# Emitting the pooling of an image one operation at a time, and new durations in the account that orders the work

## The chip, the cores and the metric

The kernel runs on one core of a Trainium2 chip. The metric is the device time of one execution in microseconds (us), as the median of several executions. For the kernel before it is 3456.73 us, from three executions between 3454.76 and 3458.35 us.

## What is computed

The input is a batch of 8 images of 256 channels and 32 x 32 pixels, all in 32-bit floats. Two layers follow one another; each adds its result to its input.

```
x = x + L0(groupnorm(x))       # layer 0: attention over pooled keys
t = tokens(x)                  # (8, 1024, 256)
t = t + attn(layernorm(t))     # layer 1: one head of 256
t = t + experts(layernorm(t))  # 8 experts, three products each, weighted by a gate
```

Layer 0 is where the change sits. Its keys and values are not those of the pixels but of four pooled maps of the image:

```
for i, r in enumerate([1, 2, 3, 6]):          # 32x32, 16x16, 11x11, 5x5
    p = einsum('bchw,ph,qw->bcpq', t, Mh, Mw) # means over windows
    p = p + depthwise3x3(p, w[i], b[i])
```

The four maps have 1024 + 256 + 121 + 25 = 1426 places. After a layer norm they are the keys and values of 8 heads of 32 channels, and the 1024 queries of an image attend to all of them. Pooling and the projection to keys and values commute, so the kernel pools the image itself and projects afterwards.

## The kernel before, in words

**The steps of attention.** For each image, each half of the heads (four heads, side by side in the array of TensorE), each half of the queries (512) and each of 12 chunks of keys, the kernel makes one *step*: 8 x 2 x 2 x 12 = 384 steps. `scores` makes four matmuls of 32 rows into a PSUM tile `sc` of four banks, of which there is one, and one exponential on ScalarE (ACT) of 128 x 2048 values into a buffer `pt`, of which there are six. `values` makes four matmuls of 32 columns from the `pt` of the step before into `pv`. After every second step, `add` (L1459) issues a transfer on the queue of GpSimd (POOL) that adds the second `pt` of a pair onto the first in memory; this is called an *adding transfer* below. A full one moves 1 MB. `sums` then adds the pairs together on VectorE (DVE), for the denominators of the softmax. A `pt` buffer is free again only when its transfer has landed and, for the first of a pair, when DVE has read it.

**The work between the steps.** Everything else runs between the steps: loading and normalising the next image, its pooling, the projections (`maps`), the depthwise taps on DVE (`convolve`), the transposes and norms of keys and values, the output projection, and all of layer 1's attention. Each of these is a generator, called a thread here. A thread yields what its next instructions need: an engine, the tiles that they read, and a PSUM tag. The work of `prepare` for an image (norm, `pool_levels`, `maps`, queries) is one thread, so what follows the pooling cannot be emitted before it. Matmuls emitted between steps by these threads are called *filler* below, since they fill TensorE (PE) while ACT works on the exponential.

**The account that sets the order.** The class `Flow` records every instruction as it is emitted (all instructions go through one helper and so show line L669 in the profile) and ties it to the one before on its engine, so that the emitted order is the order on the chip. `note` (L738) keeps an account of when each engine is next free, with the durations that `cost` (L710) gives, and of when each tile is ready. After each `scores` and after each `values`, `step` (L834) resumes every thread that is `runnable` (L807). For an engine other than PE that is the case if

```
now <= pe + AHEAD[engine]   if the inputs are ready on that engine by then
at  <= pe + NEAR[engine]    otherwise (at: when the inputs are ready)
```

where `now` is the account's time of that engine and `pe` that of PE. Filler for PE is also held to a credit: `PACE` 4.0 us a step, `PACE1` 2.0 us for the threads of layer 1. The account is not consulted on the chip; it only decides the order.

**The pooling.** `pool_levels` (L1273) makes, for each of the two halves of an image's channels, the 16 x 16 map (three operations on POOL) and the 11 x 11 map (seven). A thread yields once before each of these two groups (L1284 and L1290), and so the three, and then the seven, are emitted in one go, without an adding transfer between them. The 5 x 5 map is made by DVE (from L1304 on) in a tile `t5`, which uses the same buffer as the tiles `t2` and `t3` of the POOL operations.

**After attention.** The last of layer 1 is emitted between the first expert products; then the experts run to the end. The first products of an expert are made as plain matmuls while layer 1 is still going on, and by a scheme with seven products in place of eight afterwards.

Of the kernel before, what the change touches and what calls it, by code (L numbers as in the profile page):

```python
# [20 lines left out]
DH = 32  # L21
# [10 lines left out]
CAP = (1.5, 1.5)  # L32
NEVER = 1e9
MARGIN = 1.5
AHEAD = {"DVE": 4.0, "ACT": 2.0, "POOL": 4.0, "SP": 10.0}
NEAR = {"DVE": 1.5, "ACT": 2.0, "POOL": 1.5, "SP": 10.0}
BUFS = {"sm": 2, "sx": 1}
PACE2 = 8.0
LANDING = 9.5
# [12 lines left out]
class Kit:  # L52


    def __init__(self, nc):
        self.nc = nc
        self.n = 0
# [598 lines left out]
class Flow:  # L656
# [18 lines left out]
    def __init__(self, tc, kit):  # L675
        nc = tc.nc
        self.tc, self.kit = tc, kit
        self.now = dict.fromkeys(("PE", "DVE", "ACT", "POOL", "SP"), 0.0)
        self.last = {}
        self.ready, self.read, self.writer, self.reader, self.slots, self.open = {}, {}, {}, {}, {}, set()  # L680
        self.pe = self.Engine(self, "PE", nc.tensor)
        self.ve = self.Engine(self, "DVE", nc.vector)
        self.act = self.Engine(self, "ACT", nc.scalar)
        self.pool = self.Engine(self, "POOL", nc.gpsimd)
        self.sp = self.Engine(self, "SP", nc.sync)
        self.threads = []
        self.cut = {}
        self.also = {}
        self.credit, self.port = [0.0, 0.0], 0.0

    def tile(self, pool, shape, tag, bufs=1):
# [18 lines left out]
    def cost(self, engine, op, out, ins):  # L710
        n = 1
        for s in (out.shape if op != "bn_stats" else ins[0].shape)[1:]:
            n *= s
        if op == "tensor_reduce":
            n = 1
            for s in ins[0].shape[1:]:
                n *= s
        if "dma" in op:
            return 1.0 if engine == "POOL" else 0.4
        if engine == "PE":  # L720
            if op == "transpose":
                return 0.13
            c = max(0.2, 0.00169 * n)
            return c / 4 + 0.05 if ins[0].shape[0] <= DH or ins[0].shape[1] <= DH else c
        psum = any(i.space == PSUM for i in ins)
        if engine == "ACT":
            return 0.2 + 0.00087 * n
        if engine == "POOL":
            if n <= 64 and op == "tensor_tensor":
                return 0.3 + 0.17 * n if n <= NKC else 0.3  # L730
            return 0.15 + (0.0023 if op == "tensor_tensor" else 0.0015) * n
        if op == "reciprocal":
            return 0.1 + 0.0064 * n
        if op in ("tensor_scalar", "tensor_copy") and not psum:
            return 0.14 + 0.00065 * n
        return 0.15 + 0.00107 * n

    def note(self, engine, op, ins, args, kwargs):  # L738
        aps = [a for a in (*args, *kwargs.values()) if hasattr(a, "tensor") or hasattr(a, "space")]
        out = kwargs.get("out", args[0] if args else aps[0])  # L740
        srcs = [a for a in aps if a is not out]
        prev = self.last.get(engine)
        if prev is not None:
            self.tc.add_manual_dep(
                ins.ins,
                prev,
                mybir.DependencyInfo(mybir.DependencyClass.NoSync, mybir.DependencyReason.DATA),
                reason="program order",
            )
        self.last[engine] = ins.ins.name  # L750
        start = self.now[engine]
        names = [n for a in srcs for n in self.keys(a)]
        outs = self.keys(out)
        for n in (*names, *outs):
            if self.writer.get(n) != engine:
                start = max(start, self.ready.get(n, 0.0))
        for o in outs:
            if self.reader.get(o, engine) != engine:
                start = max(start, self.read.get(o, 0.0))
        cost = self.cost(engine, op, out, srcs)  # L760

        wide = [a for a in srcs if a.space != PSUM and a.free_size() > 4]
        if "dma" not in op and engine == "POOL" or engine == "DVE" and wide and (len(wide) > 1 or op in ("tensor_scalar", "tensor_copy")):
            start = max(start, self.port)
            self.port = start + cost
        self.now[engine] = end = start + cost
        lag = 0.15
        if "dma" in op:
            lag = 3.0 if engine == "SP" else LANDING
        for n in {*outs, self.key(out)}:  # L770
            self.ready[n] = max(self.ready.get(n, 0.0), end + lag)
            self.writer[n] = "DMA" if "dma" in op else engine
        self.open.difference_update(names)
        for n in {*names, *map(self.key, srcs)}:
            self.read[n] = max(self.read.get(n, 0.0), end + lag)
            self.reader[n] = engine
# [30 lines left out]
    def runnable(self, need, rank=0):  # L807
# [16 lines left out]
        now = self.now[engine]  # L824
        return now <= pe + AHEAD[engine] if at <= now + 0.3 else at <= pe + NEAR[engine]

# [38 lines left out]
def attention(tc, kit, f, outer, ended, nb, consts, x, t1, t2, hn, bounds, vecs, q_t, kv_t, proj_t, gqk_t, wqk, wqkv, vecs1, w1_d, w1c, gate_d, wrc, vecs2, bnvec):  # L865
# [6 lines left out]
    with ExitStack() as ctx:  # L872
# [5 lines left out]
        def T(pool, shape, tag, bufs=1):  # L878
            return f.tile(pool, shape, tag, bufs=bufs)
# [161 lines left out]
        def ve(*tiles):  # L1041
            return "DVE", tiles, None
# [4 lines left out]
        def pool(*tiles):  # L1047
            return "POOL", tiles, None
# [224 lines left out]
        def pool_levels(xi, xl):  # L1273

            img = xi.rearrange("p k (h w) -> p k h w", h=32)

            def level(s):
                n = SIDES[s]
                return xl[:, :, OFFS[s] - HW : OFFS[s] - HW + n * n].rearrange("p k (h w) -> p k h w", h=n)

            for k in range(2):
                one, l2, l3 = img[:, k], level(1)[:, k], level(2)[:, k]

                yield pool(xi)  # L1284
                t2 = T(work, [P, 32, 16], "pool")
                f.pool.tensor_tensor(t2, one[:, :, 0::2], one[:, :, 1::2], ALU.add)
                f.pool.tensor_tensor(l2, t2[:, 0::2, :], t2[:, 1::2, :], ALU.add)
                f.pool.tensor_scalar(l2, l2, 0.25, 1.0, ALU.mult, ALU.mult)

                yield pool(xi)  # L1290
                t3 = T(work, [P, 32, 11], "pool")
                f.pool.tensor_tensor(t3, one[:, :, 0::3], one[:, :, 1::3], ALU.add)
                f.pool.tensor_tensor(t3[:, :, 0:10], t3[:, :, 0:10], one[:, :, 2::3], ALU.add)
                f.pool.tensor_tensor(t3[:, :, 1:11], t3[:, :, 1:11], one[:, :, 2::3], ALU.add)
                f.pool.tensor_tensor(l3, t3[:, 0::3, :], t3[:, 1::3, :], ALU.add)
                f.pool.tensor_tensor(l3[:, 0:10, :], l3[:, 0:10, :], t3[:, 2::3, :], ALU.add)
                f.pool.tensor_tensor(l3[:, 1:11, :], l3[:, 1:11, :], t3[:, 2::3, :], ALU.add)
                flat = xl[:, k, OFFS[2] - HW : OFFS[3] - HW]
                f.pool.tensor_tensor(flat, flat, con[:, K_S11 : K_S11 + 121], ALU.mult)

            t5 = T(work, [P, 2, 32, 5], "pool")
            ends = [(i * 32 // 5, -(-(i + 1) * 32 // 5)) for i in range(5)]
            for i, (a, e) in enumerate(ends):
                yield ve(xi)  # L1304
                f.ve.tensor_reduce(t5[:, :, :, i], img[:, :, :, a:e], AX.X, ALU.add)
            yield ve(t5, xl)
            l5 = level(3)
            for i, (a, e) in enumerate(ends):
                f.ve.tensor_reduce(
                    l5[:, :, i, :], t5[:, :, a:e, :].rearrange("p k h w -> p k w h"), AX.X, ALU.add  # L1310
                )
            flat = xl[:, :, OFFS[3] - HW :]
            f.ve.tensor_tensor(flat, flat, con[:, None, K_S5 : K_S5 + 25].to_broadcast([P, 2, 25]), ALU.mult)
            pooled.append(True)

        def prepare(b):
# [32 lines left out]
            if b == 0:  # L1349
                f.spawn(pool_levels(xi, xl), 2)  # L1350
            else:
                yield from pool_levels(xi, xl)
# [435 lines left out]
        for i in range(len(steps) + 1):  # L1788
            if i < len(steps):
                b, c, half, kc = steps[i]  # L1790
# [653 lines left out]
```

## Time and profile before

| | before |
|---|---|
| time, median of 3 | 3456.73 us |
| span of the profiled execution | 3452.0 us |
| work ahead of the first step | 0 to 102 us |
| the 384 steps | 102 to 2020 us |
| last of layer 1, with the first expert products | 2020 to 2345 us |
| the other expert products | 2345 to 3452 us |
| adding transfers | 192; 160 of them move 1024 KB each, and land 7.2 us after their issue (median) |
| pooling on POOL, one image | 20 operations of 0.4 to 2.0 us |

A line of a wait reads: who waited, for whom, total us, times, longest us. A line of a timeline reads: start, duration, engine, operation, tiles written and read, shape, how many were merged, and in brackets the idle time of the engine before and what ended it. In a line of windows each engine's busy time is followed by its instructions in brackets.

### The profile page before, as it was taken

Reading aid. Unit: us, or ns where it says so; the run is one execution under the profiler, and the core shown is the slowest. Engines: PE = TensorE matmul, PEld = TensorE weight load, DVE = VectorE, ACT = ScalarE, POOL = GpSimd, SP = SyncE. Lnnn points to the kernel's source line nnn. Section 1 sums busy time; section 2 is a strip of 40 time slices with the busy share of each in tenths; the row PEclk is TensorE's granted clock in tenths of the full one; section 3 lists DMA queues with packets and bytes.
Section 4 is the critical chain, followed back from the end, with each engine's and each line's share of the span. In section 5 each row is a group of like instructions: output and inputs, shape, how many; then the busy total and the mean of one; then the engine's idle time right before and its main releaser. Section 6 shows DMA issues by size and latency. Waiting matters only on the chain.

```text
span 3452.0 us, 39939 instructions
## 1 busy us (share of the span) xinstructions
PE 3212.7 (93%) x15276; PEld 1785.8 (52%) x15276; DVE 2286.3 (66%) x3922; ACT 1673.9 (48%) x2195; POOL 496.1 (14%) x616
## 2 busy tenths in 40 slices
PE   7788889979989899999989989999999999999998
PEld 3322234425434344434434446746777777777776
DVE  6686877787888788787654534316776666666665
ACT  3566666556666566566655533342223333333332
POOL 2113131131141221321121200004000000000000
PEclk9789999999999999999999999999999999999999
DMA  1346655554554565655565754124430001000000
GB/s 48 75 102 155 144 117 111 131 132 98 137 128 101 127 135 130 137 128 121 117 143 128 150 158 164 61 79 141 140 122 19 19 19 37 19 19 19 19 13 20
DMA packets 103881, 333.28 MB, mean 97 GB/s; under 512 B 12848, under 2 KB 38200, under 8 KB 80448
## 3 DMA queue, kind: packets, MB, share of 16 engines
q0 software_dynamic: 24576, 172.51, 25.5%
q1 hardware_dynamic: 75744, 156.16, 13.2%
q8 instruction: 122, 2.00, 0.2%
q10 hardware_dynamic: 3360, 1.97, 0.2%
q14 instruction: 79, 0.65, 0.1%
HBM read 96.23 MB, written 61.87 MB: 46 GB/s over the span
## 4 chain that ended last, share of the span: by engine, by line
PE 73%; DVE 10%; DMA 6%; ACT 5%; issue 3%; POOL 2%; ACTq 0%; SPq 0%; POOLq 0%; DVEq 0%
PE bank L669 24%; PE sm L669 17%; PE y L669 11%; PE sc L669 8%; PE sx L669 6%; PE pv L669 6%; ACT pt L669 4%; DVE acc L669 4%; DMA pt<-pt 3%; DVE pt L669 1%; DVE rec L669 1%; DMA hn<-pool 1%; DMA t<-xr 1%; POOL pool L669 1%; DMA xr<-in_x_dram 1%
## 5 line engine op out<-in xcount | busy, mean ns | idle before, releaser
L669 ACT ACTIVATE pt<-sc 128x2048 f32<-128x2048 f32 (+1 forms) x384 | 720.4, 1876 | 348.0 <-PE sc L669 258.4
L669 PE MATMUL sc<-q,kn 32*128 32x512 f32 (+1 forms) x3072 | 458.3, 667 | 124.2 <-ACT pt L669 123.1
L669 DVE SCALAR_TENSOR_TENSOR acc<-p,vec,acc 128x225 f32<-128x225 f32 (+7 forms) x928 | 530.4, 578 | 39.6 <-ACT acc L669 14.9
L669 PE MATMUL bank<-h,w2e 128*128 128x512 f32 x1024 | 478.4, 593 | 0.0
L669 ACT ACTIVATE h<-bank,bnvec 128x512 f32<-128x512 f32 x298 | 229.5, 771 | 481.6 <-PE bank L669 481.6
L669 DVE TENSOR_TENSOR pt<-pt,pt 128x1024 f32<-128x1024 f32 x320 | 384.7, 1246 | 85.1 <-DMA pt<-pt 68.4
L669 PE MATMUL pv<-pt,vt 128*32 128x512 f32 (+1 forms) x3072 | 424.4, 625 | 0.0
L669 ACT ACTIVATE h<-c,bnvec 128x512 f32<-128x512 f32 x214 | 162.5, 807 | 323.2 <-DVE c L669 323.2
L669 POOL DMA_DIRECT2D pt<-pt x192 | 169.3, 882 | 975.8 <-ACT pt L669 833.5
L669 PEld LDWEIGHTS sc<-q,kn 32*128 32x128 f32 (+1 forms) x3072 | 119.1, 183 | 315.8 <-ACT pt L669 214.2
L669 DVE TENSOR_TENSOR c<-p1c,bank 128x512 f32<-128x512 f32 x107 | 73.5, 687 | 313.7 <-PE bank L669 313.7
L669 PEld LDWEIGHTS bank<-h,w2e 128*128 128x128 f32 x1024 | 194.5, 190 | 150.6 <-issue 138.1
L669 PEld LDWEIGHTS pv<-pt,vt 128*32 128x32 f32 (+1 forms) x3072 | 61.3, 109 | 311.1 <-issue 299.0
L669 POOL TENSOR_TENSOR rstd<-rstd,mhalf 128x4 f32<-128x4 f32 (+2 forms) x88 | 107.4, 1221 | 714.4 <-DVE rstd L669 586.0
L669 DVE TENSOR_TENSOR h<-h,gates 128x1024 f32<-128x1024 f32 x128 | 157.4, 1230 | 66.3 <-DMA h<-h 59.0
L669 PE MATMUL bank<-hn,w1e 128*128 128x256 f32 (+1 forms) x596 | 188.8, 446 | 10.2 <-DMA hn<-hn 10.2
L669 PE MATMUL y<-t,s3e 128*128 128x256 f32 x768 | 187.8, 381 | 0.0
L669 PE MATMUL sm<-p,v 128*128 128x256 f32 x800 | 187.0, 385 | 0.5 <-ACT sm L669 0.5
L669 PE MATMUL sm<-y,t 128*128 128x256 f32 x720 | 171.9, 385 | 6.6 <-ACT p L669 2.1
L669 PEld LDWEIGHTS sm<-p,v 128*128 128x128 f32 x800 | 149.8, 191 | 48.3 <-issue 27.7
L669 ACT ACTIVATE p<-sm 128x512 f32<-128x512 f32 (+1 forms) x149 | 87.0, 585 | 168.1 <-PE sm L669 134.8
L669 PEld LDWEIGHTS bank<-hn,w1e 128*128 128x128 f32 x596 | 114.0, 193 | 96.5 <-issue 89.7
(294 smaller groups left out, 4606.0 us busy)
## 6 DMA issues: line engine op xcount, KB each, us to landing
pt<-pt POOLq DMA_DIRECT2D x160, 1024.0 KB, 7.2
h<-h SPq DMA_DIRECT2D x72, 512.0 KB, 4.1
xi<-in_x_dram SPq DMA_DIRECT2D x16, 512.0 KB, 4.7
t<-t SPq DMA_DIRECT2D x8, 1024.0 KB, 7.8
res<-t SPq DMA_DIRECT2D x32, 256.0 KB, 4.7
t<-res SPq DMA_DIRECT2D x32, 256.0 KB, 3.1
hn<-res SPq DMA_DIRECT2D x32, 256.0 KB, 3.0
hn<-hn SPq DMA_DIRECT2D x16, 512.0 KB, 5.4
```

What stands on the lines that cost most here:

```text
L669: ins = fn(*args, **kwargs)
```

## The change

The change has four parts.

1. In `pool_levels`, a thread now yields before nearly every POOL operation: six yields more for each half of the channels. The two limits for POOL fall to 1.0 us (from 4.0 for `AHEAD` and 1.5 for `NEAR`). So pooling operations can be separated on POOL's queue, and an adding transfer can stand between them.
2. DVE's part of the pooling yields with `t5` as well, so that it is emitted only when the account says that the buffer is free of POOL's tiles.
3. `cost` has other durations: plain ACT operations, ACT operations with a scale or bias per partition, and DVE's three-operand operation.
4. PE's account knows three arrangements of the array (whole, split by rows, split by columns). A split matmul costs a quarter of a whole one, and a change of the arrangement costs 0.09, 0.2 or 0.13 us. Before, each split matmul cost a quarter and 0.05 us, and matmuls with 8 rows counted as split.

No instruction's arithmetic changes; the same instructions are emitted in another order, apart from the number of plain expert products, which depends on how far layer 1 has come.

```diff
-AHEAD = {"DVE": 4.0, "ACT": 2.0, "POOL": 4.0, "SP": 10.0}
-NEAR = {"DVE": 1.5, "ACT": 2.0, "POOL": 1.5, "SP": 10.0}
+AHEAD = {"DVE": 4.0, "ACT": 2.0, "POOL": 1.0, "SP": 10.0}
+NEAR = {"DVE": 1.5, "ACT": 2.0, "POOL": 1.0, "SP": 10.0}
@@ cost
             c = max(0.2, 0.00169 * n)
-            return c / 4 + 0.05 if ins[0].shape[0] <= DH or ins[0].shape[1] <= DH else c
+            return c if self.tiling(ins) is None else c / 4
         if engine == "ACT":
-            return 0.2 + 0.00087 * n
+            return 0.15 + 0.00084 * n + 0.16 * any(i.free_size() == 1 for i in ins[1:])
...
+        if op == "scalar_tensor_tensor":
+            return 0.23 + 0.00103 * n
...
+    @staticmethod
+    def tiling(ins):
+
+        rows, columns = ins[0].shape[0], ins[0].shape[-1]
+        return "columns" if columns <= DH and rows > 8 else "rows" if rows == DH else None
@@ note
         cost = self.cost(engine, op, out, srcs)
+        if engine == "PE":
+
+            tiling = None if op == "transpose" else self.tiling(srcs)
+            if tiling != self.tiled:
+                cost += {None: 0.09, "rows": 0.2, "columns": 0.13}[tiling]
+                self.tiled = tiling
@@ pool_levels
                 f.pool.tensor_tensor(t2, one[:, :, 0::2], one[:, :, 1::2], ALU.add)
+                yield pool(t2)
                 f.pool.tensor_tensor(l2, t2[:, 0::2, :], t2[:, 1::2, :], ALU.add)
+                yield pool(t2)
                 f.pool.tensor_scalar(l2, l2, 0.25, 1.0, ALU.mult, ALU.mult)
...
                 f.pool.tensor_tensor(t3, one[:, :, 0::3], one[:, :, 1::3], ALU.add)
+                yield pool(t3)
                 f.pool.tensor_tensor(t3[:, :, 0:10], t3[:, :, 0:10], one[:, :, 2::3], ALU.add)
+                yield pool(t3)
                 f.pool.tensor_tensor(t3[:, :, 1:11], t3[:, :, 1:11], one[:, :, 2::3], ALU.add)
+                yield pool(t3)
                 f.pool.tensor_tensor(l3, t3[:, 0::3, :], t3[:, 1::3, :], ALU.add)
                 f.pool.tensor_tensor(l3[:, 0:10, :], l3[:, 0:10, :], t3[:, 2::3, :], ALU.add)
+                yield pool(t3)
                 f.pool.tensor_tensor(l3[:, 1:11, :], l3[:, 1:11, :], t3[:, 2::3, :], ALU.add)
...
-                yield ve(xi)
+                yield ve(xi, t5)
                 f.ve.tensor_reduce(t5[:, :, :, i], img[:, :, :, a:e], AX.X, ALU.add)
```

More of the change, by code (lines that the diff above doesn't have):

```diff
@@ L688, in __init__ @@
         self.also = {}
+        self.tiled = None
         self.credit, self.port = [0.0, 0.0], 0.0
```

## The prediction

> **What bounds the kernel now.** I read the page first, for the engine with most work and for the chain that ended last.
>
> ```profile
> span 3452.0 us, 39939 instructions
> PE 3212.7 (93%) x15276; PEld 1785.8 (52%) x15276; DVE 2286.3 (66%) x3922; ACT 1673.9 (48%) x2195; POOL 496.1 (14%) x616
> PE 73%; DVE 10%; DMA 6%; ACT 5%; issue 3%; POOL 2%; ACTq 0%; SPq 0%; POOLq 0%; DVEq 0%
> ```
>
> PE has work for 93% of the span. POOL, whose order the change alters, works for 14% of it. So the change can only matter through what PE waits for. The windows tell where PE has idle time to give back.
>
> ```profile
> 102.00:2020.00 1918.00, 1747.05 (x9879) 769.34 (x9879) 1422.34 (x2514) 1172.49 (x1384) 404.50 (x475) 0.96 0.57 126
> 2345.00:3452.00 1107.00, 1084.51 (x4158) 792.80 (x4156) 701.75 (x1083) 355.07 (x555) 41.40 (x64) 0.99 0.13 47
> ```
>
> Busy times stand in the order PE, weight loads, DVE, ACT, POOL. The 384 steps leave PE idle for 1918 - 1747 = 171 us; the experts after 2345 us for 22 us, and no pooling is there. The 171 us are the ceiling. The waits within the steps split them:
>
> ```profile
> PE sc L669 <- ACT pt L669: 123.1, 97, 12.6
> ACT pt L669 <- PE sc L669: 258.4, 239, 6.5
> ACT pt L669 <- DMA pt<-pt: 60.1, 17, 12.8
> DVE pool L669 <- POOL xl L669: 54.5, 7, 13.8
> ```
>
> The first line is PE held by an exponential (the one `sc` tile is not free). I followed each of these waits one link further, to what its exponential had waited for: in 58 cases (36.6 us of PE idle) only for its own scores, so the step had too little filler; in 26 (34.8 us) it stood behind other ACT work; in 13 (42.3 us) for an adding transfer to land, because all six `pt` were taken. The third line is that last case as ACT sees it. The largest shows the mechanism:
>
> ```profile
> 725.21 1.54 POOL L669 TENSOR_TENSOR pool<-xi 128x512 f32<-128x512 f32 x1 [0.93 <-DVE xi L669]
> 730.55 3.75 POOL L669 TENSOR_TENSOR pool<-pool,xi 128x320 f32<-128x320 f32 x2
> 736.45 0.96 POOL L669 DMA_DIRECT2D pt<-pt  x1
> 744.22 1.88 ACT L669 ACTIVATE pt<-sc 128x2048 f32<-128x2048 f32 x1 [12.82 <-DMA pt<-pt]
> 746.15 2.09 PE L669 MATMUL sc<-q,kn 32*128 32x512 f32 x8 [12.56 <-ACT pt L669]
> ```
>
> POOL runs one half's ten pooling operations from 725.21 to 736.45. The transfer behind them had its data at 725.1 (the end of its exponential), is issued 11.4 us later, lands after 7.7 us, and PE stands for 12.56 us.
>
> **What the Trainium skill says.** "Advanced Engine Details and Errata", section Sequencer Loop: an engine's instructions go into that engine's queue and wait there for their semaphores. The trace agrees: the transfer leaves when the pooling ahead of it is done. "DMA: Bandwidth & Descriptors", section Anatomy of one DMA: 2.0 us and bytes/436e3, so 4.4 us for 1 MB. The trace has 7.2 us (median of 160), which I use; so delays on POOL come on top of a long landing. "SBUF — State Buffer", section SBUF: two separate sides: a GpSimd operation and a DVE operation with two SBUF inputs exclude each other. The trace agrees in size: one half's pooling takes 7.2 us beside an idle DVE (21.94 to 29.1 us) and 11.2 us above; splitting it does not shorten it. "TensorEngine Tiling (Array Packing)", section Key Properties: a change of the tiling mode drains the array. In the trace four row-split matmuls of 512 columns take 1.14 us and four column-split ones 1.07 us, while 16 whole ones take 13.73 us in the chain (0.858 us each), so a group with its change costs 0.28 or 0.21 us more than one whole matmul.
>
> ```profile
> 2263.83 13.73 PE bank L669 x32
> ```
>
> **The change part by part.** Both kernels can be built, and the listing of their instructions by engine tells what moves; durations are those of before.
>
> *The adding transfers.* Before, pooling stands ahead of 12 transfers within the steps, each time 7.7 us of it by the mean durations (1.32 + 0.87 + 0.45 + 0.85 + 2 x 1.12 + 0.6 + 2 x 0.4 + 0.6). After, the same 12 x 7.7 = 92 us stand ahead of 25 transfers, in pieces of 0.5 to 9.1 us; 7.7, 6.4, 9.1 and 6.4 are left at 6 us or more, together 30 of 92 us. Of the 13 PE waits above, four wait for a transfer that had pooling ahead: 1.80 us (at 329), 2.70 (520), 4.28 (528), 12.56 (746), together 21.3 us. The other eight delayed transfers made PE wait for nothing, since the steps there had filler. If the waits go with the pooling left in large pieces, a third stays: **-14 us** (bounds: -21, all; -7, if pieces of 4 us hurt as well).
>
> *DVE's wait for the buffer.* 54.5 us of DVE idle, of which 17 lie ahead of the first step. There DVE is on the path (it ran taps from 33 to 62 us without a pause), and the changed listing puts two large taps (1.22 and 1.25 us) before the reduces, inside the 13.84 us wait: **-2.5 us** (bounds 0 and -6). The other 37 us lie beside 1918 - 1422 = 496 us of idle DVE and PE's own filler; I cost them at nothing beyond the 4.28 us wait counted above.
>
> *Filler.* The new account spreads filler otherwise. By columns at 0.858/512 us each, steps with under 1 us of filler number 99 before and 108 after; what they lack to 1 us sums to 67.6 and 75.8 us. A step without filler shows 1.0 us of PE idle (the commonest wait of PE in the list), so **+8 us**. Bounds: +4, as the 58 waits for scores alone cost 36.6 us of the 67.6 that are lacking (half; the rest is taken by other waits), and +10, one us for each of ten more steps with next to no filler (under 0.3 us: 57 and 67).
>
> *Work.* Plain first products number 23 instead of 21; the seventh-product scheme saves an eighth of 4 x 0.858 us, so 2 x 0.43 = **+0.9 us**. Changes of the array's arrangement fall from 1141 to 1124: 17 x 0.14 (mean of the account's three prices) = **-2.4 us**. The other durations in the account issue nothing; they are in the two counts above. The added yields add no instruction and no wait on the chip; where pooling is later, `maps` of that image is queued behind it: its end moves from step 38 to 50, 80 to 92, 125 to 136, 169 to 176, 209 to 218 and 256 to 262.
>
> *Redrawn waits.* Some 18 other PE waits of 2 to 6 us each within the steps (64 us together, 3.5 in the mean) depend on coincidences of the order. In a new order they fall anew; taken as independent, that is sqrt(18) x 3.5 = 15 us either way.
>
> Sum: -14 - 2.5 + 8 + 0.9 - 2.4 = -10 us, so **3447 us**.
>
> **The rivals.**
>
> *Deeper (3410 us).* Truer durations also end the other waits for transfers: all 42.3 us, with -2.5 and -2.4. For it: the account plans with 9.5 us for a landing, more than the 7.2 measured, so truer durations elsewhere could space the steps to fit. Against it: the nine other transfers stand behind `rstd` and `diag` operations, or are issued at once and only land late; no edit splits those.
>
> *Given back (3454 us).* The lack of filler costs what the transfers gain: -7 - 2.5 + 8 + 0.9 - 2.4 = -3 us. For it: 92 us of pooling now delays twice as many transfers, each a little.
>
> *Slower (3467 us).* Later pooling squeezes the second image. Its keys, in three parts, come in steps 45, 51 and 55, where they are needed in 48, 52 and 56; before, in 39, 45 and 50. If DVE lags the account by one step (5 us), PE stands at one of these places, +5, and the redraw falls badly, +15, on top of -10: +10. Against it: the next image has six steps of margin, later ones more, and DVE is idle for 26% of the steps.
>
> **How the numbers follow.** Likeliest case 0.52, deeper 0.12, given back 0.17, slower 0.19. Faster by over 0.2% (below 3450): nearly all of the likeliest with its redraw, and the deeper, 0.62. Within 0.2%: 0.18. Slower: 0.20. The range: the likeliest less the redraw and the better bounds, 3447 - 15 - 7 - 3.5 - 4 = 3417, up to the slower case and a smaller part of the doubt on the transfers' gain (5 of 7 us), 3472.
>
> **What would show it.** Right: waits of ACT for adding transfers fall from 60 to about 35 us, none over 8 us; DVE's wait for POOL falls from 54.5 to under 20; PE's idle in the steps falls from 171 to about 160; exponentials held only by scores rise by some 10 cases; the experts' stretch keeps 1107 us. Wrong: an ACT wait of over 10 us for a transfer, waits of PE for late keys near steps 48 to 56, or idle of PE that moves from transfers to filler-poor steps one for one. That the redraw is as large as the effect is what most endangers this prediction.

## The result and the profile after

The kernel after takes 3414.99 us in the median (3410.68 to 3420.16), the kernel before 3457.19 us beside it. The ratio is 0.9879, with a 95% interval of 0.9862 to 0.9897: 42 us or 1.2% faster. I had predicted 3447 us, 10 us less than before, and a range from 3417. The direction is right; the size is a quarter of what was measured, and the time lies 2 us below the range.

The page of after answers the three lines shown of before (span, busy time by engine, the chain that ended last):

```profile
span 3418.4 us, 39922 instructions
PE 3204.7 (94%) x15264; PEld 1781.8 (52%) x15264; DVE 2285.8 (67%) x3914; ACT 1675.6 (49%) x2193; POOL 499.0 (15%) x616
PE 74%; DMA 5%; ACT 4%; DVE 2%; issue 2%; POOL 1%; SPq 0%; ACTq 0%; DVEq 0%; POOLq 0%
```

The engines' work is the same within 0.6%. PE is busy for 8 us less, and PE's busy time is no constant, as will be seen. Most of the difference is idle time of PE. The windows of after, in the order of the columns as before (width, PE, weight loads, DVE, ACT, POOL, granted clock, DMA share, GB/s):

```profile
102.00:2020.00 1918.00, 1764.65 (x9978) 786.12 (x9977) 1440.14 (x2526) 1179.70 (x1397) 410.08 (x476) 0.96 0.58 129
2345.00:3418.00 1073.00, 1059.39 (x4070) 772.99 (x4068) 680.12 (x1056) 347.87 (x542) 12.21 (x19) 0.99 0.14 47
```

The same stretch of 1918 us holds 1765 us of PE work where it held 1747. The last step starts at 1975.5 us instead of 2017.7, 42 us earlier, and the first at 102.5 instead of 102.3. What follows the last step takes 1442.8 us, 8.6 more than before; part of the steps' gain is filler that moved behind them. Now the waits of after, in the form of before (who waited, for whom, us, times, longest):

```profile
PE sc L669 <- ACT pt L669: 114.0, 95, 7.1
ACT pt L669 <- PE sc L669: 244.7, 231, 6.9
ACT pt L669 <- DMA pt<-pt: 45.6, 15, 8.0
DVE pool L669 <- POOL xl L669: 20.4, 6, 5.4
```

ACT's waits for adding transfers fall from 60.1 to 45.6 us, the longest from 12.8 to 8.0; DVE's wait for the pooling buffer from 54.5 to 20.4 us. Followed one link further, as in the prediction, PE's waits for `sc` divide so:

| the exponential had waited for | before, us (cases) | after, us (cases) |
|---|---|---|
| a transfer with pooling ahead of it | 21.3 (4) | 3.5 (2) |
| a transfer behind `rstd` or `diag` | 13.5 (7) | 9.9 (7) |
| a transfer that only landed late | 7.5 (2) | 18.0 (4) |
| its own scores alone | 34.5 (56) | 44.8 (63) |
| other ACT work ahead of it | 34.8 (26) | 23.4 (19) |
| something else; of it DVE, which had still to read a `pt`: 4.2 and 10.4 | 12.5 (11) | 15.8 (14) |
| PE's waits in the steps that aren't for `sc` | 46.8 | 27.8 |

The rows for `sc` add up to some 1 us more than the 123.1 and 114.0 us of the views, which leave out waits of under 0.15 us.

The pooling of the same image on POOL's timeline of after (start, duration, tiles, shape; DMA_DIRECT2D is an adding transfer):

```profile
751.53 1.03 POOL L669 TENSOR_TENSOR pool<-xi 128x512 f32<-128x512 f32 x1
752.64 1.14 POOL L669 TENSOR_TENSOR xl<-pool 128x256 f32<-128x256 f32 x1
753.73 0.91 POOL L669 DMA_DIRECT2D pt<-pt  x1
...
766.57 0.86 POOL L669 DMA_DIRECT2D pt<-pt  x1
767.20 1.08 POOL L669 TENSOR_TENSOR pool<-xi 128x352 f32<-128x352 f32 x1
768.35 2.05 POOL L669 TENSOR_TENSOR pool<-pool,xi 128x320 f32<-128x320 f32 x2
...
775.09 0.92 POOL L669 DMA_DIRECT2D pt<-pt  x1
```

Transfers now stand between the operations. They need not be far apart in number: from 767.20 to 775.09 eight operations still follow one another. But PE waited for nothing there.

**Where the 42 us are.** I split each span into PE's idle time (without some 11 us ahead of its first instruction and in its shortest gaps), work lost to a lower clock, and the rest. For the second term: the records show the granted clock of TensorE as 1 or 0.5, never between, and half of PE's busy time in the 0.5 stretches is counted as lost.

| profiled execution, us | span | PE idle | lost at clock 0.5 | rest |
|---|---|---|---|---|
| before | 3452.0 | 227.9 | 61.6 | 3162.5 |
| after | 3418.4 | 202.2 | 57.3 | 3158.9 |

Of 33.6 us in these two executions, 25.7 are idle time (27.7 of it in the steps, 2.0 given back elsewhere), 4.3 are clock, 3.6 are the rest. The rest term is nearly one number for all kernels with the same work, so the split can be trusted to a few us.

### The profile page after: what moved, and what is told of

The parts are those of the page before. It is cut to its first block, busy times and chain, and to the rows that moved or that the text cites. A ratio compares the mean times of both kernels' runs of the same rounds, so it can differ in the third digit from the quotient of the medians.

```text
span 3418.4 us, 39922 instructions
## 1 busy us (share of the span) xinstructions
PE 3204.7 (94%) x15264; PEld 1781.8 (52%) x15264; DVE 2285.8 (67%) x3914; ACT 1675.6 (49%) x2193; POOL 499.0 (15%) x616
## 4 chain that ended last, share of the span: by engine, by line
PE 74%; DMA 5%; ACT 4%; DVE 2%; issue 2%; POOL 1%; SPq 0%; ACTq 0%; DVEq 0%; POOLq 0%
PE bank L669 25%; PE sm L669 18%; PE y L669 11%; PE sc L669 8%; PE sx L669 6%; PE pv L669 6%; ACT pt L669 3%; DMA pt<-pt 2%; DMA t<-xr 1%; DMA xr<-in_x_dram 1%; DVE acc L669 0%; DMA hn<-hn 0%; DVE pt L669 0%; DVE rec L669 0%; DVE xr L669 0%
## 5 line engine op out<-in xcount | busy, mean ns | idle before, releaser
L669 PE MATMUL sc<-q,kn 32*128 32x512 f32 (+1 forms) x3072 | 452.4, 659 | 115.5 <-ACT pt L669 114.0
L669 DVE SCALAR_TENSOR_TENSOR acc<-p,vec,acc 128x225 f32<-128x225 f32 (+7 forms) x928 | 528.5, 576 | 35.7 <-ACT acc L669 11.2
L669 PE MATMUL sm<-p,v 128*128 128x256 f32 x736 | 173.8, 388 | 6.1 <-DVE xr L669 6.1
L669 PEld LDWEIGHTS sm<-p,v 128*128 128x128 f32 x736 | 139.3, 193 | 49.7 <-issue 24.4
```

The costliest lines, as they stand in the source:

```text
L669: ins = fn(*args, **kwargs)
```

## The experiments

**First: is it the pooling that delays the transfers?** My theory was the transfers' term: pooling ahead of adding transfers costs the kernel before some 14 us. In `thin_pooling` the order of before stays, instruction for instruction, but from the second image on each pooling operation handles a few rows only. Most of the pooled maps are left out; the account still books the full durations, so nothing else moves.

```diff
+            def op(name, rows, *args):
...
+                few = [a[:, 0:rows] if hasattr(a, "shape") else a for a in args]
+                f.note("POOL", name, getattr(f.pool.eng, name)(*few), args, {})
...
-                f.pool.tensor_tensor(t2, one[:, :, 0::2], one[:, :, 1::2], ALU.add)
+                op("tensor_tensor", 2, t2, one[:, :, 0::2], one[:, :, 1::2], ALU.add)
```

> The kernel before in its own order, instruction by instruction; but from the second image on each pooling operation on POOL works on a few rows of its tiles only (most of the pooled maps of these images are left out, the account still books the full durations). A block of ten pooling operations ahead of an adding transfer shrinks from 7.7 us to about 4. Theory A (pooling ahead of the transfers makes PE wait): the four PE waits of 21.3 us go, and with them the stretches of half clock that follow them (about 6 us of lost work): -27 us, 3430. Theory B (the transfers would land late anyway, or the waits pop up elsewhere): within 5 us of before. Theory C (the gain is a lucky order): the order is that of before, so 3457 less at most the 21 us.

Measured: 3436.53 us, ratio 0.9953 [0.9936, 0.9969], so 16 us less than before (interval 11 to 22). PE's waits for transfers with pooling ahead fall from 21.3 us to 13.0. What is left is mostly one case, the old one of 746 us, which now stands at 728; the timeline of `thin_pooling`:

```profile
709.16 1.88 ACT L669 ACTIVATE pt<-sc 128x2048 f32<-128x2048 f32 x1 [0.82 <-ACT att L669]
711.08 0.74 POOL L1286 TENSOR_TENSOR pool<-xi 128x32 f32<-128x32 f32 x1 [0.93 <-DVE xi L669]
712.39 1.25 POOL L1286 TENSOR_TENSOR pool<-xi 128x66 f32<-128x66 f32 x1
718.56 0.96 POOL L669 DMA_DIRECT2D pt<-pt  x1 [0.27 <-issue]
726.20 1.88 ACT L669 ACTIVATE pt<-sc 128x2048 f32<-128x2048 f32 x1 [8.82 <-DMA pt<-pt]
728.13 2.09 PE L669 MATMUL sc<-q,kn 32*128 32x512 f32 x8 [8.56 <-ACT pt L669]
```

The transfer has its data at 711.04, the end of the exponential, and is issued at 718.56. Ten operations of 11 to 66 elements take 7.2 us here (11.2 in before), so this kernel takes away a part of the delay only: 4 of 12.56 us at this place, 8.3 us of PE's waits in all. The first step starts at 98.7 us instead of 102.3 (3.6 us), and the work lost to the clock falls by 3.5. The experiment shows that time of POOL in the pooling is on PE's path in the order of before, with these 16 us for the part that was taken away. It doesn't part the ways by which it gets there: DVE's wait for the pooling buffer falls as well, from 54.5 to 27.3 us.

**Second: the parts alone.** `pool_only` is before with the new yields (`t5` among them) and limits, and the old account. `account_t5` is before with the new durations, the array's arrangements and DVE's yield with `t5`; the pooling stays in its two groups. `after_no_durations` is after with the old durations for ACT and DVE.

```diff
+++ pool_only
-AHEAD = {"DVE": 4.0, "ACT": 2.0, "POOL": 4.0, "SP": 10.0}
+AHEAD = {"DVE": 4.0, "ACT": 2.0, "POOL": 1.0, "SP": 10.0}
...
+                yield pool(t2)
+++ account_t5
-            return 0.2 + 0.00087 * n
+            return 0.15 + 0.00084 * n + 0.16 * any(i.free_size() == 1 for i in ins[1:])
...
-                yield ve(xi)
+                yield ve(xi, t5)
```

> The kernel before with the edits of the pooling alone (yields, the two limits of POOL, the wait for t5), the old durations and the old price of split matmuls. Theory A (pooling ahead of transfers): -27 us from it, give or take 15 for the new order: about 3430. Theory of the account (the new durations and prices space the work better and carry most of the gain): about 3450. Theory C (any new order gains or loses some 15 us): anywhere from 3425 to 3460.

> The kernel before with the new durations and the new prices of the array's arrangement, and DVE's wait for t5 (without it no such kernel can be built), but pooling emitted in its old groups under the old limits. Theory A: pooling still stands ahead of transfers in groups of 3 to 13, so most of the 27 us stay: about 3450. Theory of the account: most of the gain is here: about 3425.

> The changed kernel with the old durations for ACT and for the three-operand operation of DVE; pooling edits and the prices of the array's arrangement are kept. If the pooling carries the gain and the rest is noise of the order: 3425, give or take 8. If the durations are needed for the last 10 us: 3425 and no less. If the prices of the arrangement give them: 3415.

| | us | ratio to before, 95% |
|---|---|---|
| `pool_only` | 3424.6 | 0.9915 [0.9898, 0.9932] |
| `account_t5` | 3465.3 | 1.0032 [1.0020, 1.0045] |
| `after_no_durations` | 3460.2 | 1.0011 [1.0002, 1.0019] |

The waits of ACT in the steps and of DVE, of `pool_only` first and then of `account_t5`:

```profile
ACT pt L669 <- DMA pt<-pt: 23.5, 9, 6.0
DVE pool L669 <- POOL xl L669: 8.4, 5, 3.1
```

```profile
ACT pt L669 <- DMA pt<-pt: 73.6, 18, 8.2
DVE pool L669 <- POOL xl L669: 10.6, 6, 3.6
```

Where the pooling is split, ACT waits for transfers for 23.5 us, and PE's share from pooling is 3.5 us; where it stays in groups, it is 73.6 us, and 28.5 us of PE's idle. So in these two orders the waits that the splitting is meant for go with it and stay without it. DVE's wait goes in both, since both have the `t5` yield: that wait is the yield's part, and it doesn't decide the time, for `account_t5` is the slower one. The times don't add up, however: -29 and +12 make -17, not -42. And `after_no_durations` has the split pooling, but none of the gain: its profiled execution has 233.7 us of idle and 66.7 us lost to the clock, against 202.2 and 57.3 in after. Taken as a test of the durations, it would say that durations, which issue nothing, are worth 45 us. I took that as a sign that any new order is worth something like it, either way.

**Third: is it the splitting on the queue itself?** `regrouped` keeps the order of after on every engine but POOL. Only there, the ten operations of a half are issued together, when the last of them is due. If the gain comes from transfers between pooling operations, it must go.

```diff
-                f.pool.tensor_tensor(t2, one[:, :, 0::2], one[:, :, 1::2], ALU.add)
+                op("tensor_tensor", t2, one[:, :, 0::2], one[:, :, 1::2], ALU.add)
                 yield pool(t2)
...
+                f.booked = True
+                f.pool.tensor_tensor(t2, one[:, :, 0::2], one[:, :, 1::2], ALU.add)
+                f.pool.tensor_tensor(l2, t2[:, 0::2, :], t2[:, 1::2, :], ALU.add)
...
+                f.booked = False
```

> The changed kernel in its own order on every engine but POOL: the account books the pooling operation by operation as the change does, but the ten operations of one half are issued together, when the last of them is due. So only the groups of ten ahead of adding transfers come back, in the changed kernel's order. Theory A: the pooling's waits of PE come back, 15 to 20 us with the half clock after them: 3430 to 3435. Theory C (the gain is the lucky order of the other engines): the order is kept, so 3415 to 3420.

Measured: 3420.65 us, ratio 0.9899 [0.9883, 0.9916], where after has 0.9879 [0.9862, 0.9897]. That is 6 to 7 us over after, and the two intervals together allow for 15 us or for nothing. The groups are there, as POOL's timeline of `regrouped` shows (first and last of one half's ten operations, and the transfers about them; then the exponential that the second transfer waits for):

```profile
784.07 0.92 POOL L669 DMA_DIRECT2D pt<-pt  x1 [0.21 <-issue]
784.70 1.37 POOL L669 TENSOR_TENSOR pool<-xi 128x512 f32<-128x512 f32 x1
...
792.20 0.40 POOL L669 TENSOR_TENSOR xl<-xl,con 128x121 f32<-128x121 f32 x1
792.76 0.89 POOL L669 DMA_DIRECT2D pt<-pt  x1 [0.17 <-issue]
...
787.82 1.88 ACT L669 ACTIVATE pt<-sc 128x2048 f32<-128x2048 f32 x1 [0.50 <-PE sc L669]
```

And the waits of the steps:

```profile
PE sc L669 <- ACT pt L669: 116.9, 97, 7.5
ACT pt L669 <- DMA pt<-pt: 43.9, 15, 8.2
```

Thirteen transfers are issued 6 us or more after their data (after: 8, before: 15), and PE waits for pooling for 0.3 us. But pooling fills that time in only four of the thirteen. The group above stands ahead of a transfer whose data came at 789.70 us, when most of the group was done, so it delays it by 3 us and not by 8. Summed over all transfers, pooling ran for 43 us between a transfer's data and its issue, against 40 in after and 68 in before. So `regrouped` brings back the groups and hardly their delays. Its longest three, 6.9 to 7.5 us of pooling ahead of a transfer, cost PE next to nothing in this order, where three of 8.5 to 10.6 us in before cost 19.5 us (the waits of 2.70, 4.28 and 12.56 us). Theory C is nearer than theory A by the time, but whether the gain comes from transfers between pooling operations, or from where the pooling is put among the steps, this experiment can't tell.

**Fourth: how much of 42 us is any new order worth?** The rival to every reading above is that an order is a draw. I made new draws of both kernels: one number of the account changed a little, `LANDING` (L39, the account's time for a landing) or `MARGIN` (L34, used in `runnable`). Neither removes an operation or means to help.

```diff
-LANDING = 9.5
+LANDING = 9.4
```

> The kernel before with MARGIN 1.45 in place of 1.5, so that the order comes out anew. Pooling stands ahead of transfers in groups of ten as before. Theory A (pooling in groups of ten ahead of transfers costs some 20 us of waits and the half clock after them): 3450 to 3465, as in the first redraw (3459). Theory C (luck): 3425 to 3470.

> The kernel before with one number of the account moved by a hundredth: a landing is booked with 9.4 us in place of 9.5. It means nothing, but the order comes out anew. It shows how large an effect an arbitrary new order has. If the redraw is 15 us: 3440 to 3472. If orders of one account differ by little: within 5 us of 3457.

> The changed kernel with one number of the account moved without meaning (MARGIN 1.45 in place of 1.5), so that the order comes out anew. If the changed kernel's 3415 is what this account and this pooling give: 3410 to 3422. If some 10 us of it, beyond the 3425 of the pooling edits alone, were a lucky order: 3425 or more.

> The changed kernel with a landing booked at 9.4 us in place of 9.5, again without meaning. The same two outcomes: 3410 to 3422 if the 3415 is the account's, 3425 or more if it was luck. PE's waits in the steps other than for the sc tile were 46.8 us before and 27.8 us in the changed kernel: luck says that they return to 40 or more.

> The kernel before with MARGIN 1.55 in place of 1.5, a new order without meaning. Redraws of before gave 3459 and 3427, so a spread of some 15 us about 3447 is expected, 3430 to 3465, with 13 to 21 us of PE's waits behind pooling.

> The changed kernel with MARGIN 1.55 in place of 1.5. Redraws of the changed kernel gave 3447 and 3402. If the redraw is wider than thought, with a spread of 20 us about 3425: 3405 to 3445.

> The kernel before with a landing booked at 9.6 us. Orders of before gave 3457, 3459, 3427 and 3467; 3435 to 3470 is expected.

> The changed kernel with a landing booked at 9.6 us. The same: 3405 to 3445. If the change itself carries most of the 42 us, the mean of all its orders stays at or under 3425 and some 30 us under that of before's orders; if it was mostly luck, the two means come within 15 us.

> The kernel before with a landing booked at 9.45 us. Five orders of before gave 3427 to 3467, mean 3450; another draw of the same: 3430 to 3470. If the change is worth some 22 us on the average, the two means stay 15 to 30 us apart with these two.

> The changed kernel with a landing booked at 9.45 us. Five orders of the changed kernel gave 3402 to 3449, mean 3427; another draw of the same: 3405 to 3450.

| edit | before, us (ratio, 95%) | after, us (ratio, 95%) |
|---|---|---|
| none | 3457.2 | 3415.0 (0.9879 [0.9862, 0.9897]) |
| `MARGIN` 1.45 | 3427.5 (0.9914 [0.9897, 0.9930]) | 3447.0 (0.9975 [0.9967, 0.9983]) |
| `MARGIN` 1.55 | 3466.7 (1.0030 [1.0015, 1.0046]) | 3424.2 (0.9910 [0.9891, 0.9930]) |
| `LANDING` 9.4 | 3459.5 (1.0019 [1.0009, 1.0029]) | 3402.5 (0.9845 [0.9829, 0.9861]) |
| `LANDING` 9.45 | 3473.0 (1.0044 [1.0028, 1.0060]) | 3447.2 (0.9975 [0.9961, 0.9989]) |
| `LANDING` 9.6 | 3439.9 (0.9952 [0.9937, 0.9967]) | 3448.5 (0.9979 [0.9972, 0.9987]) |
| mean (sd) | 3454 (17) | 3431 (20) |

An edit of 1% or less (`LANDING`) moves after by up to 34 us and before by up to 17; one of 3% (`MARGIN`) moves either by up to 32. The fastest, after with `LANDING` 9.4, beats both kernels with 3402.5 us.

The means differ by 23 us. With the two spreads its standard error is sqrt(17^2/6 + 20^2/6) = 11 us, so the 95% interval is about 0 to 47 us. The best estimate is that some 23 of the 42 us belong to the change; after is a draw 16 us better than its own mean, before one 3 us worse than its own. The five redraws of each, without the first row, differ by 19 us (interval -9 to 48), so they don't show by themselves that the time falls. Of the two outcomes set out for the means (30 us apart with after at or under 3425, or within 15 us), neither came. Term by term over the profiled executions (means of six):

| us | before | after | difference |
|---|---|---|---|
| PE idle, all | 221.5 | 210.0 | -11.5 |
| of it: transfers with pooling ahead | 15.6 | 3.3 | -12.3 |
| transfers that only landed late | 11.2 | 16.7 | +5.5 |
| scores alone (too little filler) | 35.2 | 47.9 | +12.7 |
| waits in the steps that aren't for `sc` | 46.9 | 29.5 | -17.3 |
| lost at clock 0.5 | 68.5 | 57.7 | -10.8 |
| rest | 3162.5 | 3160.1 | -2.4 |
| span | 3452.5 | 3427.8 | -24.7 |

The rows "of it" are the ones that bear on the argument, not all. Two numbers are steadier than the time. One is what the splitting acts on: pooling runs for 68 to 83 us between a transfer's data and its issue in the six orders of before, and for 34 to 45 us in the six of after (means 77 and 40). The other: the 384 steps take 1916 us in the mean (sd 17) before, and 1878 us (sd 4) after. The stretch behind them grows by 14 us, 12 of them PE work that moved there. So the steps are shorter by 38 us in the mean, and a third of that is work put off.

**Fifth: what does a wait of PE cost?** The clock's term was in neither my sum nor my rivals. Around the 12.56 us wait of before at 746 us, the windows (same columns; the granted clock is third from the end):

```profile
738.00:746.00 8.00, 0.00 (x0) 0.00 (x0) 7.73 (x9) 1.78 (x1) 7.51 (x10) 0.50 1.03 208
746.00:749.40 3.40, 3.25 (x16) 0.92 (x20) 0.45 (x1) 1.19 (x2) 1.13 (x3) 0.50 0.59 120
749.40:753.00 3.60, 3.60 (x24) 0.67 (x20) 0.52 (x1) 1.61 (x4) 1.97 (x2) 0.72 0.36 73
```

After the wait the four matmuls of `sc` (each shows as two in the trace) took 2.09 us, where those of the step before took 1.14:

```profile
731.45 1.14 PE L669 MATMUL sc<-q,kn 32*128 32x512 f32 x8 [1.05 <-ACT pt L669]
...
746.15 2.09 PE L669 MATMUL sc<-q,kn 32*128 32x512 f32 x8 [12.56 <-ACT pt L669]
```

To price it apart, I put waits into the experts of after, where PE otherwise has none: a small product waits for a chain of copies on ACT, begun when an earlier product is done. `price_long` makes ten waits with 6 copies, `price_longer` ten with 13; `price_short` was to make forty short ones.

```diff
+            if late:
+                for _ in range(13):
+                    f.act.activation(held[0], held[0], AF.Copy)
+                f.act.activation(held[0][:, :2], before[0][:, :2], AF.Copy)
+                f.pe.matmul(ps[:, :2], lhsT=held[0][:, :P], rhs=held[0][:, :2], start=True, stop=True)
...
+                half(h, w2[e], e, src, 2, 3, m, m == 1 and i in range(40, 120, 8))
```

> The changed kernel with 40 short waits of PE put into the experts' part, where PE has work throughout: the second product of every other block of work from the 40th on waits for one ACT operation on the first (about 1.3 us each, 50 us in all); some small matmuls are added. If a wait costs its length and no more: +50 us, 3465. If each wait of PE also draws a stretch of half clock: +50 and 40 x 2 us or more, over 3540.

> The same with 10 long waits of about 4.8 us (six more ACT operations ahead of each), 48 us in all. If a wait costs its length and no more: +48 us, 3463. If waits of over 2 us draw a stretch of half clock, as nearly all of them did in the traces so far, of 3.4 to 6.8 us with some 2 us of lost work each: +68 us, 3483.

> The changed kernel with ten waits of PE put into the experts' part, of about 6 us each (13 ACT operations ahead of each; the run with six gave waits of 2.57 us, of which 3 of 10 drew a stretch of half clock). If a wait costs its length alone: +60 us over 3415. If each also draws a stretch of 3.4 to 6.8 us of half clock, of which PE works through 3 us or more: +60 and another 15 to 30 us, 3490 to 3505.

`price_short` (3420.4 us) tells nothing: other products ran in between, and the forty waits did not come about. `price_long`: 3451.6 us, 37 over after; its waits were 2.57 us each but for one of 2.94, where 4.8 were meant, and 3 of the 10 were followed by a half-clock stretch. `price_longer`: 3508.6 us, ratio 1.0153 [1.0136, 1.0170], 94 us over after. Its waits add 72 us of idle; each is followed by a stretch of half clock. One of them in its windows and its timeline:

```profile
2570.00:2577.70 7.70, 0.14 (x2) 0.00 (x1) 0.00 (x0) 7.26 (x13) 0.00 (x0) 0.78 0.00 0
2577.70:2581.10 3.40, 3.40 (x6) 1.85 (x7) 0.00 (x0) 0.00 (x0) 0.00 (x0) 0.50 0.00 0
2581.10:2584.40 3.30, 3.30 (x15) 2.72 (x15) 1.32 (x2) 1.05 (x2) 0.00 (x0) 1.00 0.02 5
```

```profile
2565.24 1.88 PE L669 MATMUL bank<-h,w2e 128*128 128x512 f32 x4
...
2577.70 0.58 PE L669 MATMUL bank<-held 128*128 128x2 f32 x2 [7.56 <-ACT held L669]
2578.14 3.43 PE L669 MATMUL bank<-h,w2e 128*128 128x512 f32 x4
```

The same two products (four matmuls in the trace) take 1.88 us and 3.43 us. The stretch of 3.40 us is all busy, so 1.7 us are lost: ten times that is 17 of the 94 us, beside 72 of idle and a few for the added products. (Outside the steps, `price_longer` loses 17.7 us more to the clock than after.) A wait of 7.2 us cost about 9 here.

## Why the prediction was right in direction and wrong in size

**What bounds the kernel.** Right: the gain came from PE's idle time in the steps, 170.9 to 143.2 us, of the 171 us that I had called the ceiling. The step that was incomplete is the reading of the windows. The line of the steps that I showed has the clock 0.96 in it, and I counted PE's busy time as work. Of 1747 us "busy" in the steps of before, 53 are lost to half clock. The Trainium skill had it: "TensorE: Matmul & The Clock Gate", section What's actually happening, describes two states of the clock, the lower one at half, entered after an idle window of some 3.4 us; its section HAM oscillation counts half of the throttled time as lost. The trace agrees with the half (two equal products took 1.88 and 3.43 us), and it has the 3.4 us as the grid on which the clock changes. It differs in what is needed: about 2 us of PE idle within one cell of that grid were enough (last section). The split of the 123.1 us of waits for `sc` was incomplete too: the three classes that I gave add up to 113.7, and most of the waits for something else (12.5 us in the table above) are missing from them.

**The transfers, -14 us.** Right in size. In these two executions the waits with pooling ahead fell by 17.8 us, over the six orders of each by 12.3, and `thin_pooling` gives 16 us without any new order, 8.3 of them in these waits. The reason that I gave holds as far as that the delays shrink: pooling between a transfer's data and its issue falls from 68 to 40 us, and from 77 to 40 in the means of six. The prediction had kept 92 us on both sides, in smaller pieces; it counted the pooling that stands ahead in the order, not what runs after the data is there. That it is the cutting on the queue which does it, and not the place among the steps, isn't shown: `regrouped` puts the pieces together again, loses some 7 us (none to 15), but brings back few of the delays. That ACT's waits for transfers would fall to about 35 us was too much; they fell to 45.6, and PE's waits for transfers that only land late rose from 7.5 to 18.0 us.

**DVE's wait and the prefix, -2.5 us.** Wrong, with nothing in its place: the wait fell nearly as forecast, to 20.4 us, but the first step starts at 102.5 us instead of 102.3. The two taps did run inside the wait (at 26.24 us), but the reduces behind them then start at 30.67 us instead of 28.70, again after a wait for POOL, and nothing was gained at the first step. The other 37 us, costed at nothing, were indeed worth nothing that I can find: `account_t5` lost the wait and is slower.

**Filler, +8 us.** Right in kind and nearly in size: waits for scores alone rose by 10.3 us in these two executions (7 more cases, where I said 10) and by 12.7 in the means.

**Work, -1.5 us.** Right within what can be told: the rest term fell by 3.6 us, in the means by 2.4, and it holds more than these two items. The experts' stretch took 8.6 us more behind the last step than before, where I had said that it stays; filler moved there.

**Missing from the sum.** This is the step that put the centre wrong: terms that I set at nothing. First the clock, -4.3 us here, -10.8 in the means. Second the waits in the steps that aren't for `sc` (for `xr`, `pool`, `acc` and others): -19 us here, -17.3 in the means (before 32 to 59 us, after 19 to 38). Third, the other way, transfers that only land late: +5.5 in the means. I had counted the second only as part of the redraw, and the clock nowhere. In the means the terms that I did price come to -12.3 + 0 + 12.7 - 2.4 = -2 us instead of -10, and those left out to -22.6. So the direction came out right mostly through terms that weren't in the sum. That is luck, but for the part of the clock's term that goes with the transfers' waits, which no run parts from the rest. Why the second shrinks I did not isolate; it may be that threads which are no longer held behind a whole group of pooling hand PE its inputs earlier, but no run shows that.

**The redraw, 15 us.** This is the step that put the range wrong, by its size and by its place. I took 18 waits of 3.5 us as independent. The measured spread of an order is 17 us before and 20 after. In before it lies in the steps (sd 17, behind them 3), in after behind them (sd 19, in the steps 4), where I had put nothing. And the range took one such draw of one sigma, less the better bounds, down to 3417. From what the runs show, the centre was 16 us too high (3447 for 3431, the mean of after's orders), and the draw of after gave another 16, which is luck. A range for 8 times in 10 around this change needs 1.28 x 20 = 26 us on both sides for the draw alone.

**The rivals.** *Deeper* has the nearest time (3410 us), but not by its reason: waits for transfers behind `rstd` or `diag` or for a late landing didn't end, they went from 21.0 to 27.9 us. *Given back* is wrong by its time and in these two executions, where transfers gained 17.8 us and filler lost 10.3; over the six orders its reason came true (12.3 gained, 12.7 lost), and it is the unpriced terms that made the change pay. *Slower* is wrong: no wait of PE for the keys of the second image appears. What I called the greatest danger, that the redraw is as large as the effect, is what happened.

**What stays open.** How much exactly is the change's own: 0 to 47 us with six orders each. Whether the cutting of the pooling or its place among the steps makes the gain. And whether the new durations help: with split pooling, the old ones gave 3460 us in one order (`after_no_durations`) and 3425 in another (`pool_only`, which has the old price of split matmuls too), and the new ones 3431 in the mean of six. By these the durations can't be told from the draw.

## What to carry to other kernels

Where an account or a scheduler decides the order, compare two versions over several orders each, made by edits that mean nothing; one order of each can show 42 us where 23 are the change's, or the other sign. Before pricing an edit by the waits that it removes, test in a fixed order (thin the work, keep the places), and test the other way round (put the work back, keep the new order), and then look whether the delay that was meant came back with it. Count PE's idle time and its work at half clock separately: a long wait costs more than its length.

## What the runs showed of the hardware that I had not expected

- The clock of TensorE in these records is 1 or 0.5, and 151 to 223 us of each of the twelve spans are at 0.5, in 20 to 32 stretches. Over the twelve orders, a stretch was on within 1.5 us after 162 of 164 PE waits of over 3.4 us (without the one that opens each execution), 64 of 78 of 2.6 to 3.4 us, 34 of 48 of 2.0 to 2.6 us, 23 of 183 of 1.2 to 2.0 us, and 78 of 1067 of 0.15 to 1.2 us.
- What decides is not the length of one wait. In these twelve executions and the two of `price_long` and `price_longer`, all 748 changes of the clock lie on a grid of 3.413 us that is fixed within an execution, so that stretches last 3.4, 6.8, 10.2 or 13.7 us. In the twelve orders, all 226 cells of the grid at full clock in which PE was idle for over 2.0 us in all were followed by a cell at half clock; of the 11,124 other cells, 96 were. The ten waits of `price_long` show it: the three that drew a stretch had 1.92, 2.04 and 2.17 us of idle in one cell; of the seven others, six had at most 1.30 to 1.76 us in one cell, and one 2.01.
- A wait of 7.2 us in a stretch that is otherwise busy cost 9 us (`price_longer`, ten waits, 94 us).
- The pooling operation of 66 elements took 1.25 us at 712.39 us and 0.29 at 723.24 in `thin_pooling`; the ten of one half took 7.2 us at 711 us and 3.9 us at 721 us.
- A group of ten pooling operations on the queue ahead of a 1 MB transfer delays it only by what runs after its data is there: 10.6 us of pooling in before at 736 us (PE waited for 12.56 us), and 3 us of a group of 8 us in `regrouped` at 784 us.
